# Layer 1's feed-forward: rows sent to one of two experts through DRAM, in place of both experts on all rows

## Chip, core and metric

The kernel runs on one core of one Trainium2 chip. The metric is the device time of one execution in microseconds. A core has five engines with a queue each, all executing in order: PE (TensorE, matrix products), ACT (ScalarE), DVE (VectorE), POOL (GpSimd) and SP (SyncE, which here only issues DMAs). They meet through semaphores.

## The reference

A four-layer decoder on `x` of 128 sequences x 64 rows x 128 features, that is 8192 rows, in float32. Each layer adds a cross-attention over `ctx_1024` and a feed-forward part to `x`, both on the normalised rows. The part that the change touches is layer 1's feed-forward:

```python
gate_scores = xf @ gate_w.T                       # two scores a row
top1 = jnp.argmax(softmax(gate_scores), axis=-1)
one_hot = jax.nn.one_hot(top1, 2)
masked = xf[None, :, :] * one_hot.T[:, :, None]   # a row's copy is zero for the expert it isn't sent to
h = relu(einsum('end,edh->enh', masked, w1) + b1[:, None, :])     # 128 -> 512
expert_out = einsum('enh,ehd->end', h, w2) + b2[:, None, :]       # 512 -> 128
routing_output = expert_out.sum(axis=0)
shared = relu(xf @ sw1 + sb1) @ sw2 + sb2
return routing_output + shared
```

The expert that a row isn't sent to still adds a constant row, `relu(b1) @ w2 + b2`. The other layers: layer 0 mixes eight one-matrix experts densely, layer 2 sends each row to one of seven gated experts beside a shared one, layer 3 has a mixed-projection attention.

## The kernel before

The 8192 rows are 16 groups (`NG`) of 512 rows, each held in SBUF as `xg[g]`, four tiles of 128 rows by 128 features. For each group the program records the operations of six stages: layer 0 attention (`x0`), layer 0 feed-forward (`l0f`), layer 1 attention (`x1`), layer 1 feed-forward (`l1f`), layer 2 attention (`x2`) and layer 2's routing (`route`). Then follow, for two halves of the groups (12 and 4), layer 2's expert blocks (`table`, `block`, `shared`, `gather`) and layer 3 (`l3x`, `mix`, `l3f`).

Nothing runs in recorded order. Each `op(engine, duration, function, reads, writes, priority, ...)` goes into a planner (`Plan`, L162 on), which places all operations of all groups on the five engines by estimated durations, dependencies, buffer slots and priority, and then emits each engine's instructions in that order. The order of every queue is fixed when the program is built. A group's base priority is `10 * g`, plus `SKEW` (15) a stage, plus an offset by stage, operation and engine from the table `PRI`. An operation with `alt` may go to a second engine: normalisation (`ln_xn`, L555), evacuations (`copy_out`, L588) and the rectification in `l1f` go to ACT or DVE, bias rows (`add_row`, L607) to POOL or DVE. So the 16 groups' stages overlap: one group's attention fills the engines while another's feed-forward waits.

Buffers are in pools (`spec`): `c` holds a group's transposed context, `k`, `q` and `o` attention operands, `fx` and `fm` transposed rows, `p` transposed probabilities, `mx` row maxima. `b` is four PSUM banks. `h` is a view of 14 tiles of `hbig`; layer 2's block weights (`wt`) and the hidden tiles `h2` are views of the same storage, and `fw` (3072 columns) holds all of layer 1's weights and, later, layer 2's shared weights. The list `mark["l1f"]` holds the last operations of layer 1's feed-forward; layer 2's weight loads wait for all of them.

`l1f(g)` normalises the rows (`xn`), transposes them (`xnT`), and adds the sum of both experts' and the shared output bias (`add_row`). `logits` gives two scores a row, `choose` (L1095) the 0/1 choice. POOL multiplies `xn` by the choice (L1105), PE transposes the product (`m1T`), and POOL subtracts it from `xnT` (`m0T`, L1115). Then 12 up-projections of 128 hidden features each follow (L1125), over all 512 rows: four of the shared expert on `xnT`, four of expert 1 on `m1T`, four of expert 0 on `m0T`. Each is rectified with its bias (L1134 on ACT, L1136 on DVE) into an `h` tile. For each of the four row tiles, 12 down-projections add up in PSUM (L1144); DVE adds the result to `xg[g]` (L1151).

In attention, the score product reads a key operand (`kbd`) that SP's four DMAs fill from `k` (`fill_kbd`, L652), POOL subtracts the row maximum (`shift`, L794), ACT takes the exponential (L785), PE transposes the probabilities (L809).

Layer 2 already sends rows through DRAM: `route` writes rows with indirect DMAs from POOL into `xs_d` (L1249), `block` loads weights and rows at addresses that SP reads from a table in SBUF (L1410, L1414), and `gather` fetches results with indirect DMAs (L1454).

Of the kernel before, what the change touches and what calls it, by code (L numbers as in the profile page):

```python
# [11 lines left out]
F32 = mybir.dt.float32  # L12
# [31 lines left out]
FW = 3072  # L44
# [15 lines left out]
S_LEN = S_E + E2  # L60
# [5 lines left out]
SKEW, SKEW3, ALT, WINDOW = 15.0, 12.0, 1.160527449, 0.268996472  # L66
# [5 lines left out]
    "block0 block <lambda> 4": -4, "block0 block tr 0": 37, "block0 dma fn 4": 30.5,  # L72
    "block0 swiglu <lambda> 0": 3.5, "block0 swiglu <lambda> 1": 35.5, "block0 swiglu <lambda> 2": -1,
    "block0 swiglu down 0": 20, "block1 block <lambda> 1": 13.5, "block1 block <lambda> 4": -12.5,
    "block1 block tr 0": -22.5, "block1 dma fn 4": 71, "block1 swiglu <lambda> 0": 4,
    "block1 swiglu <lambda> 1": 41, "block1 swiglu <lambda> 2": -32, "block1 swiglu down 0": 1,
    "gather0 gather <lambda> 3": 3.5, "gather0 gather fn 2": 6.5, "gather0 stats fn 2": -0.5,
    "gather1 gather <lambda> 3": 78, "gather1 gather fn 2": 29.5, "gather1 stats fn 2": -3.5,
    "l0f copy_out fn 1": 3, "l0f l0f <lambda> 0": 9, "l0f l0f <lambda> 1": 9.5, "l0f l0f <lambda> 2": -145,
    "l0f l0f acc 2": -123.5, "l0f l0f eb 0": 46.5, "l0f l0f g1 2": 43.5, "l0f l0f g2 2": 41.5,  # L80
    "l0f ln_xn fn 1": 17.5, "l0f logits fn 0": 18.5, "l0f pow_rs fn 3": -4, "l0f stats fn 2": -39,
    "l0f transpose4 fn 0": 59.5, "l1f add_row <lambda> 3": 12.5, "l1f copy_out fn 1": -43.5,
    "l1f l1f <lambda> 0": 196, "l1f l1f <lambda> 2": 55.5, "l1f l1f <lambda> 3": 48, "l1f l1f choose 2": 11.5,
    "l1f l1f down 0": 360, "l1f l1f relu 1": 32, "l1f ln_xn fn 1": -12, "l1f logits fn 0": 5, "l1f pow_rs fn 3": 7,
    "l1f stats fn 2": 0.5, "l1f transpose4 fn 0": 45.5, "l3f0 attend av 0": 41.5, "l3f0 attend tr 0": -4.5,
    "l3f0 copy_out fn 1": -52, "l3f0 dma fn 4": -9.5, "l3f0 exp_ <lambda> 1": 25, "l3f0 fill_kbd fn 4": 56,
    "l3f0 l3f <lambda> 1": 2, "l3f0 l3f <lambda> 2": 17, "l3f0 l3f <lambda> 3": 106, "l3f0 l3f b_v 3": 51.5,
    "l3f0 l3f evac 1": -131, "l3f0 l3f load 4": -2, "l3f0 l3f project 0": -36.5, "l3f0 l3f put 2": -15,
    "l3f0 maximum fn 2": 40, "l3f0 normalise fn 2": 4, "l3f0 out_proj <lambda> 2": 36, "l3f0 out_proj fn 0": 11,
    "l3f0 scores fn 0": -58, "l3f0 shift fn 3": -1, "l3f1 attend av 0": 1, "l3f1 attend tr 0": -22,  # L90
    "l3f1 copy_out fn 1": 8.5, "l3f1 dma fn 4": -3, "l3f1 exp_ <lambda> 1": 14, "l3f1 fill_kbd fn 4": -18,
    "l3f1 l3f <lambda> 1": -2, "l3f1 l3f <lambda> 2": -13.5, "l3f1 l3f <lambda> 3": 4, "l3f1 l3f b_v 3": 9.5,
    "l3f1 l3f evac 1": 12.5, "l3f1 l3f load 4": -13.5, "l3f1 l3f project 0": -58, "l3f1 l3f put 2": -8,
    "l3f1 maximum fn 2": 4, "l3f1 normalise fn 2": -2, "l3f1 out_proj <lambda> 2": 4, "l3f1 out_proj fn 0": -4.5,
    "l3f1 scores fn 0": -26, "l3f1 shift fn 3": -6.5, "l3x0 add_row <lambda> 3": 8, "l3x0 copy_out fn 1": -36,
    "l3x0 dma fn 4": 61.5, "l3x0 l3x <lambda> 1": 166, "l3x0 l3x <lambda> 2": -5.5, "l3x0 l3x <lambda> 3": -10.5,
    "l3x0 l3x av 0": 28.5, "l3x0 l3x norm 2": -21.5, "l3x0 l3x sc 0": 7, "l3x0 l3x sums 2": 33,
    "l3x0 l3x tr 0": -17.5, "l3x0 ln_xn fn 1": 14, "l3x0 pow_rs fn 3": 12, "l3x0 stats fn 2": 9,
    "l3x0 transpose4 fn 0": 15, "l3x1 add_row <lambda> 3": 3.5, "l3x1 copy_out fn 1": -38, "l3x1 dma fn 4": 97,
    "l3x1 l3x <lambda> 1": 36.5, "l3x1 l3x <lambda> 2": 8, "l3x1 l3x <lambda> 3": -2, "l3x1 l3x av 0": 13.5,  # L100
    "l3x1 l3x sc 0": 26, "l3x1 l3x sums 2": -28.5, "l3x1 l3x tr 0": 7.5, "l3x1 ln_xn fn 1": -1,
    "l3x1 pow_rs fn 3": -3, "l3x1 stats fn 2": -1, "l3x1 transpose4 fn 0": -1, "mix0 add_row <lambda> 3": 26.5,
    "mix0 copy_out fn 1": -64, "mix0 ln_xn fn 1": -3.5, "mix0 mix <lambda> 0": 54.5, "mix0 mix <lambda> 1": 18.5,
    "mix0 mix <lambda> 2": -29.5, "mix0 mix b3mm 0": 37.5, "mix0 mix choose 2": 81, "mix0 mix put 2": 27.5,
    "mix0 mix spread_ 0": 101, "mix0 mix weigh 2": -76, "mix0 pow_rs fn 3": -17.5, "mix0 transpose4 fn 0": 38,
    "mix1 add_row <lambda> 3": 42, "mix1 copy_out fn 1": -14.5, "mix1 ln_xn fn 1": 3.5, "mix1 mix <lambda> 0": 16,
    "mix1 mix <lambda> 1": 10.5, "mix1 mix <lambda> 2": -26.5, "mix1 mix b3mm 0": 1.5, "mix1 mix choose 2": 5.5,
    "mix1 mix put 2": 28, "mix1 mix spread_ 0": 15.5, "mix1 mix weigh 2": -25.5, "mix1 pow_rs fn 3": 2.5,
    "mix1 transpose4 fn 0": -0.5, "route copy_out fn 1": -98.5, "route dma fn 4": 0.5, "route ln_xn fn 1": 51.5,
    "route pow_rs fn 3": 13, "route route <lambda> 1": 2, "route route <lambda> 2": -25,  # L110
    "route route <lambda> 3": 48.5, "route route count 0": -3, "route route r2 2": -22, "route route r3 2": 8,
    "route route r4 2": 11.5, "route route r5 2": -1.5, "route route take 2": -4.5, "route stats fn 2": -19.5,
    "route transpose4 fn 0": 7, "shared0 copy_out fn 1": 10.5, "shared0 ln_xn fn 1": 10.5,
    "shared0 shared fn 2": 11.5, "shared0 swiglu <lambda> 0": 11, "shared0 swiglu <lambda> 1": 8.5,
    "shared0 swiglu <lambda> 2": 7, "shared0 swiglu down 0": 20.5, "shared0 transpose4 fn 0": 3.5,
    "shared1 copy_out fn 1": -16, "shared1 ln_xn fn 1": 24, "shared1 shared fn 2": -7,
    "shared1 swiglu <lambda> 0": 11, "shared1 swiglu <lambda> 1": -2.5, "shared1 swiglu <lambda> 2": 1,
    "shared1 swiglu down 0": 6.5, "shared1 transpose4 fn 0": 21.5, "table0 table <lambda> 0": 26,
    "table0 table b1 2": -3.5, "table0 table b2 2": 28, "table1 table <lambda> 0": 16, "table1 table b1 2": 2,
    "table1 table b2 2": 9.5, "x0 add_row <lambda> 3": 27, "x0 attend av 0": -6, "x0 attend tr 0": 9.5,  # L120
    "x0 attention <lambda> 2": -1.5, "x0 attention <lambda> 3": 26, "x0 copy_out fn 1": -102, "x0 dma fn 4": 504.5,
    "x0 exp_ <lambda> 1": -9, "x0 fill_kbd fn 4": -5, "x0 ln_xn fn 1": 19.5, "x0 maximum fn 2": 70,
    "x0 normalise fn 2": -88.5, "x0 out_proj <lambda> 2": -40.5, "x0 out_proj fn 0": -25.5, "x0 pow_rs fn 3": 4,
    "x0 proj <lambda> 0": 32.5, "x0 proj fn 1": -32, "x0 scores fn 0": 12, "x0 shift fn 3": -2,
    "x0 stats fn 2": -30, "x0 transpose4 fn 0": 10, "x0 vproj evac 1": -2, "x0 vproj fn 0": 73,
    "x1 attend av 0": 33, "x1 attend tr 0": 6.5, "x1 attention <lambda> 2": -35, "x1 attention <lambda> 3": 11,
    "x1 copy_out fn 1": -28.5, "x1 dma fn 4": 501.5, "x1 exp_ <lambda> 1": 10, "x1 fill_kbd fn 4": 5,
    "x1 ln_xn fn 1": 95.5, "x1 maximum fn 2": 10.5, "x1 normalise fn 2": -46.5, "x1 out_proj <lambda> 2": -103,
    "x1 out_proj fn 0": -1, "x1 pow_rs fn 3": 2, "x1 proj <lambda> 0": 24, "x1 proj fn 1": -1,
    "x1 scores fn 0": 83.5, "x1 shift fn 3": -14, "x1 stats fn 2": -15.5, "x1 transpose4 fn 0": 8,  # L130
    "x1 vproj evac 1": -1, "x1 vproj fn 0": 9.5, "x2 add_row <lambda> 3": 0.5, "x2 attention <lambda> 2": -46,
    "x2 attention <lambda> 3": 90.5, "x2 copy_out fn 1": -11.5, "x2 dma fn 4": 506, "x2 fill_kbd fn 4": 3.5,
    "x2 ln_xn fn 1": -3, "x2 out_proj <lambda> 2": -34, "x2 out_proj fn 0": -0.5, "x2 pow_rs fn 3": 8,
    "x2 product fn 0": -45, "x2 proj <lambda> 0": -13, "x2 proj fn 1": -9.5, "x2 scores fn 0": -13,
    "x2 stats fn 2": -15.5, "x2 transpose4 fn 0": 29, "x2 vproj_by_batch evac 2": -93.5,
    "x2 vproj_by_batch fn 0": -44, " b2_row b2_row 2": 2.5, " dma fn 4": 497, " lambda <lambda> 0": 32.5,
    " lambda <lambda> 2": -29.5, " lambda <lambda> 3": 14.5, " rel_mm rel_mm 0": -11.5,
# [162 lines left out]
def kernel(ctx: ExitStack, tc: tile.TileContext, a: dict, out: bass.AP):  # L300
# [90 lines left out]
    def tl(r):  # L391
        return kinds[r.tag][r.slot]
# [1563 lines left out]
```

## Time and profile before

| | us |
|---|---|
| median of 21 runs | 1990.86 |
| lowest and highest of them | 1983.95, 1999.85 |
| the profiled execution | 1993.57 |
| span of its instructions | 1991.8 |
| POOL's indirect scatter (L1249), mean of 64 | 0.989 |
| POOL's indirect gather (L1454), mean of 64 | 1.004 |
| rectification of 128x512 on ACT (L1134), mean of 164 | 0.685 |
| the same on DVE (L1136), mean of 28 | 0.741 |

Engine times in the text are of this one execution. A "group" of the profile is all instructions with the same line, engine and tiles; its row gives their busy time and the mean of one. In rows with a bar the first number after it is busy time, the second the mean in ns, the last part the idle time of the engine just before them and what ended it.

### The profile page before, as it was taken

Reading aid. Unit: us, or ns where it says so; the run is one execution under the profiler, and the core shown is the slowest. Engines: PE = TensorE matmul, PEld = TensorE weight load, DVE = VectorE, ACT = ScalarE, POOL = GpSimd, SP = SyncE. Lnnn points to the kernel's source line nnn. Section 1 sums busy time; section 2 is a strip of 40 time slices with the busy share of each in tenths; the row PEclk is TensorE's granted clock in tenths of the full one; section 3 lists DMA queues with packets and bytes.
Section 4 is the critical chain, followed back from the end, with each engine's and each line's share of the span. In section 5 each row is a group of like instructions: output and inputs, shape, how many; then the busy total and the mean of one; then the engine's idle time right before and its main releaser. Section 6 shows DMA issues by size and latency. Waiting matters only on the chain.

```text
span 1991.8 us, 66420 instructions
## 1 busy us (share of the span) xinstructions
PE 1807.9 (91%) x27506; PEld 1305.3 (66%) x27506; DVE 1547.7 (78%) x4023; ACT 1083.0 (54%) x2032; POOL 1021.0 (51%) x1331
## 2 busy tenths in 40 slices
PE   7778999999998999999999999999998987888885
PEld 5544756765765666765666667778756776676664
DVE  5989897878798987798987864445577878988666
ACT  2545755555555565556564553343445666666554
POOL 5635745464555654557644471020388768855231
PEclk8989999999999999999999999999999999989898
DMA  6200001011001010001001012444424576545461
GB/s 186 80 13 26 27 26 30 13 30 40 24 29 46 28 32 29 27 27 50 29 24 33 23 42 79 133 128 121 121 75 127 155 245 188 172 151 178 158 190 54
DMA packets 139229, 158.73 MB, mean 80 GB/s; under 512 B 40836, under 2 KB 98096, under 8 KB 138928
## 3 DMA queue, kind: packets, MB, share of 16 engines
q1 hardware_dynamic: 134832, 146.09, 24.1%
q0 software_dynamic: 4096, 8.40, 1.5%
q8 instruction: 216, 3.54, 0.7%
q14 instruction: 85, 0.70, 0.1%
HBM read 121.66 MB, written 15.99 MB: 69 GB/s over the span
## 4 chain that ended last, share of the span: by engine, by line
PE 48%; DVE 26%; POOL 8%; issue 8%; ACT 4%; DMA 3%; SPq 3%; POOLq 0%; DVEq 0%; ACTq 0%
PE b L1353 8%; PE b L1144 5%; PE b L809 4%; POOL s L794 4%; DVE x L1078 4%; PE b L1125 4%; PE b L1382 4%; DVE mx L779 4%; PE S L755 4%; PE b L1068 3%; PE b L638 3%; PE b L821 2%; PE b L1734 2%; PE b L864 2%; PE b L583 2%
## 5 line engine op out<-in xcount | busy, mean ns | idle before, releaser
L794 POOL TENSOR_TENSOR s<-s,mx 128x512 f32<-128x512 f32 x320 | 323.7, 1044 | 224.9 <-DVE mx L779 187.7
L593 ACT COPY p<-b 128x512 f32<-128x512 f32 x370 | 199.0, 591 | 144.4 <-PE b L809 127.6
L809 PE MATMUL b<-ident,s 128*128 128x128 f32 x1536 | 216.5, 291 | 48.7 <-ACT s L785 35.0
L785 ACT ACTIVATE s<-s 128x2048 f32<-128x2048 f32 x96 | 183.8, 1914 | 111.2 <-POOL s L794 82.3
L809 PEld LDWEIGHTS b<-ident,s 128*128 128x128 f32 x1536 | 180.2, 149 | 93.1 <-ACT s L785 54.0
L563 ACT ACTIVATE xn<-x,nmr,rstd 128x128 f32<-128x128 f32 x472 | 194.4, 488 | 26.2 <-POOL nmr L548 24.9
L1078 DVE SCALAR_TENSOR_TENSOR x<-b,gt,x 128x128 f32<-128x128 f32 x512 | 177.9, 347 | 30.2 <-PE b L1068 13.9
L544 POOL TENSOR_SCALAR ve<-mv 128x4 f32<-128x4 f32 x144 | 34.8, 242 | 320.0 <-DVE mv L538 305.0
L755 PE MATMUL S<-kbd,q 32*64 32x256 f32 x4096 | 151.7, 401 | 46.4 <-DMA kbd<-k 22.5
L1144 PEld LDWEIGHTS b<-fw,hbig 128*128 128x128 f32 x1536 | 178.0, 192 | 10.4 <-issue 9.4
L779 DVE TENSOR_REDUCE mx<-s 128x32 f32<-128x2048 f32 x80 | 181.8, 2274 | 3.5 <-ACT s L1786 2.9
L1144 PE MATMUL b<-fw,hbig 128*128 128x128 f32 x1536 | 183.9, 277 | 0.0
L1370 DVE TENSOR_TENSOR hbig<-fm,b 128x256 f32<-128x256 f32 (+2 forms) x180 | 85.3, 486 | 101.2 <-ACT fm L1365 74.5
L1134 ACT ACTIVATE hbig<-b,cols 128x512 f32<-128x512 f32 x164 | 111.3, 685 | 84.2 <-PE b L1125 83.4
L1068 PE MATMUL b<-mats,fx 128*128 128x512 f32 x256 | 140.0, 629 | 1.8 <-DVE x L1078 1.5
L545 POOL TENSOR_TENSOR rstd<-ve,mhalf 128x4 f32<-128x4 f32 x128 | 133.6, 1044 | 10.7
L755 PEld LDWEIGHTS S<-kbd,q 32*64 32x64 f32 x4096 | 82.2, 136 | 86.8 <-DMA kbd<-k 21.9
L1353 PE MATMUL b<-fx,hbig 128*128 128x256 f32 (+1 forms) x528 | 128.9, 393 | 4.2 <-ACT fx L1441 1.0
L1365 ACT ACTIVATE fm<-b 128x256 f32<-128x256 f32 (+2 forms) x180 | 76.5, 438 | 100.8 <-PE b L1353 92.0
L821 PEld LDWEIGHTS b<-p,vaug 128*32 128x32 f32 x6144 | 97.9, 112 | 50.0 <-issue 24.3
L821 PE MATMUL b<-p,vaug 128*32 128x64 f32 x6144 | 124.1, 226 | 6.3 <-issue 4.1
L1125 PE MATMUL b<-fm,fw 128*128 128x512 f32 x256 | 125.1, 606 | 0.6 <-DVE x L1078 0.3
(292 smaller groups left out, 3870.6 us busy)
## 6 DMA issues: line engine op xcount, KB each, us to landing
fw<-in_l_w SPq DMA_DIRECT2D x64, 384.0 KB
vaug<-in_l_w SPq DMA_DIRECT2D x64, 384.0 KB
hbig<-in_l_w SPq DMA_DIRECT2D x44, 544.0 KB
c<-in_ctxT SPq DMA_DIRECT2D x64, 256.0 KB
kbd<-k SPq DMA_DIRECT2D x256, 64.0 KB
q<-xs_d SPq DMA_DIRECT2D x44, 128.0 KB
ys_d<-o SPq DMA_DIRECT2D x44, 128.0 KB
x<-in_x SPq DMA_DIRECT2D x32, 128.0 KB
```

What stands on the lines that cost most here:

```text
L563: A.activation(y[:, t, :], xg[g][:, t, :], AF.Identity, bias=nmr[:, g, n], scale=rstd[:, g, n])
L593: A.copy(tl(dst), tl(b))
L755: T.matmul(ps[64 * i : 64 * i + 64, r, u * 256 : u * 256 + 256], lhsT=qT[row, 64 * b : 64 * b + 64], rhs=kbd[row, :, 64 * b : 64 * b + 64] ...
L779: V.tensor_reduce(tl(mxr), heads(y), AX.X, ALU.max)
L794: G.tensor_tensor(y, y, bc(tl(mxr)[:, h], 2, [P, n, S]), ALU.subtract)
L809: T.transpose(tl(b)[:, r * P : (r + 1) * P], tl(s)[:, c : c + P], ident)
L821: T.matmul(tl(po)[32 * r : 32 * r + 32, c : c + 64], lhsT=vaugs[kv.slot][:, w0 : w0 + 32], rhs=tl(ps[p])[:, r * P + 64 * i : r * P + 64 * ...
L1068: lambda t=t, u=u, pe=pe: T.matmul(tl(pe), lhsT=tl(xnT)[:, t * P : (t + 1) * P], rhs=mats[:, M_E0 + 4 * u : M_E0 + 4 * u + 4, :], start=Tr ...
L1078: V.scalar_tensor_tensor(xg[g][:, t, :], tl(pe)[:, e * D : (e + 1) * D], w[:, t, 4 * u + e : 4 * u + e + 1], xg[g][:, t, :], ALU.mult, ALU ...
L1125: lambda n=n, src=src, ph=ph: T.matmul(tl(ph), lhsT=fw[:, n * P : (n + 1) * P], rhs=tl(src), start=True, stop=True),
L1144: T.matmul(tl(py)[:, t * P : (t + 1) * P], lhsT=tl(hs[n])[:, t * P : (t + 1) * P], rhs=w2f[:, n, :], start=(n == 0), stop=(n == 11),)
L1353: T.matmul(tl(ps)[0:n, at : at + m], lhsT=w()[:, off + c * P : off + c * P + n], rhs=tl(xT)[:, 0:m], start=True, stop=True,)
```

## The change

Layer 1's feed-forward is cut in three. Groups are taken in pairs (1024 rows).

- `l1f(g)` normalises and transposes as before. `choose` now also finds each row's place: rows for expert 0 count from the start of a 1024-row DRAM tile (`x1_d`), rows for expert 1 from its end. A count matmul ranks rows across partitions, `place` writes the addresses, and four indirect DMAs on POOL scatter the normalised rows. On the odd group of a pair, `table1` works out which of the first four blocks of 256 rows is whose. `unsent` adds the constant difference row `cd`, made once in `zeros`, to the rows whose unsent expert is expert 0. The shared expert (4 up, 16 down) runs on `xnT` at once (`up_down`).
- `l1b(n)` runs five blocks of 256 rows for pair `n`. SP reads the block's expert from the table, loads that expert's weights (128 x 1028) and the rows; two transposes, four ups, four rectifications, eight downs; ACT copies the result and SP stores it to `y1_d`. Four blocks cover the tile in order, and the fifth is the block in which the two experts meet, computed a second time with expert 1.
- `l1c(g)` fetches the results with four indirect DMAs and adds them to `xg[g]` on POOL or DVE.

Stages `x2` and `route` of both groups of a pair are recorded after the pair's `l1c`. The table `PRI` (shortened away below), `ALT` and `WINDOW` hold other numbers, some of the planner's durations differ, the loads of `tri` and `srt` have priority 16 in place of 40, and several pools are of other sizes.

```diff
-FW = 3072
+FW = 3080
+HID1, B1 = 512, 256
+N1 = 2 * GT
+NB1 = N1 // B1 + 1
+W1 = HID1 + 4 * D + 4
...
-SKEW, SKEW3, ALT, WINDOW = 15.0, 12.0, 1.160527449, 0.268996472
+SKEW, SKEW3, ALT, WINDOW = 15.0, 12.0, 1.493905422, 0.159761594
...
-        "c": (2, [P, GT]), "q": (2, [P, GT]), "k": (3, [P, GT]), "o": (3, [P, GT]),
-        "xnT": (1, [P, GT]), "xn": (2, [P, GT]), "fx": (2, [P, GT]), "fm": (4, [P, GT]), "p": (5, [P, GT]),
-        "s": (2, [P, 2048]), "m": (2, [P, 256]), "mb": (3, [P, 256]), "mx": (12, [P, 32]), "tn": (1, [P, 288]),
-        "st": (4, [P, TP * 6]), "gt": (2, [P, 264]),
-        "rt": (1, [P, 400]),
+        "c": (1, [P, GT]), "q": (2, [P, GT]), "k": (2, [P, GT]), "o": (3, [P, GT]),
+        "xnT": (1, [P, GT]), "xn": (2, [P, GT]), "fx": (4, [P, GT]), "fm": (3, [P, GT]), "p": (4, [P, GT]),
+        "s": (2, [P, 2048]), "m": (2, [P, 256]), "mb": (2, [P, 256]), "mx": (6, [P, 32]), "tn": (1, [P, 288]),
+        "st": (7, [P, TP * 6]), "gt": (3, [P, 264]),
+        "rt": (2, [P, 400]),
...
+    kinds["w1"] = [fw[:, HID1 + 4 * D + i * W1 : HID1 + 4 * D + (i + 1) * W1] for i in range(2)]
...
     def l1f(g, pri):
         xn, xnT = layer_norm(g, pri, "fx")
         add_row(g, R_B20, pri)
...
+            V.tensor_copy(pos.unsqueeze(2), gs[:, :, 0:1])
+            V.tensor_tensor(sel.unsqueeze(2), gs[:, :, 1:2], pos.unsqueeze(2), ALU.is_gt)
+            V.tensor_copy(on, sel)
+            V.tensor_tensor(
+                y, srt[:, S_TRI : S_TRI + 20].rearrange("p (i t) -> p i t", t=TP), bc(on, 1, [P, 5, TP]), ALU.mult
+            )
+            V.tensor_reduce(pre, y, AX.X, ALU.add)
...
+        def count():
+            T.matmul(tl(rank)[:, 0:1], lhsT=tri, rhs=pre[:, 4:5], start=True, stop=not k)
...
+        def place():
+            V.tensor_tensor(pos, pos, tl(rank)[:, 0:1].to_broadcast([P, TP]), ALU.subtract)
+            V.tensor_copy(ip.bitcast(I32), pos)
...
+        def scatter(t):
+            w = G.indirect_dma_start(
+                out=x1_d[n], out_offset=bass.IndirectOffsetOnAxis(ap=ip[:, t : t + 1].bitcast(I32), axis=0),
+                in_=g4(tl(xn))[:, t, :], in_offset=None,
+            )
...
+            G.memset(scrap, 0.0)
...
+        def unsent():
+            for t in range(TP):
+                V.scalar_tensor_tensor(xg[g][:, t, :], cd, sel[:, t : t + 1], xg[g][:, t, :], ALU.mult, ALU.add)
...
+    def l1b(n, pri):
...
+        for j in range(NB1):
+            wt, xb, xbT = Res("w1"), Res("q"), Res("fx")
+            last = j == NB1 - 1
+
+            def weights(j=j, wt=wt, last=last):
+                at = P if last else register(tab1[0:1, n, j : j + 1], P)
+                SY.dma_start(out=tl(wt), in_=a["l1_we"][bass.ds(at, P), :])
+
+            def rows_in(j=j, xb=xb, last=last):
+                at = register(tab1[0:1, n, 4:5], N1 - B1) if last else j * B1
+                SY.dma_start(
+                    out=view(tl(xb)[:, 0:B1]), in_=x1_d[n][bass.ds(at, B1), :].rearrange("(t p) d -> p t d", p=P)
+                )
...
+    def l1c(g, pri):
+        yg = Res("k")
+        for t in range(TP):
+            op(
+                POOL, 1.0,
+                lambda t=t: G.indirect_dma_start(
+                    out=g4(tl(yg))[:, t, :], out_offset=None, in_=y1_d[g // 2],
+                    in_offset=bass.IndirectOffsetOnAxis(ap=l1cell(g, L_YP + t, 1).bitcast(I32), axis=0),
+                ),
...
+    for g in range(NG):
+        stats(g, 10.0 * g - 0.5)
+        stages(g, enumerate((0, l0f, 1, l1f)))
+        if g % 2:
+            plan.stage = "l1b"
+            l1b(g // 2, 10.0 * g + SKEW * 3 + 3)
+            for i in (g - 1, g):
+                plan.stage = "l1c"
+                l1c(i, 10.0 * g + SKEW * 3 + 6)
+                stages(i, ((4, 2), (5, route)))
```

The up- and down-projections, for the shared expert (`m` = 512) and for a block (`m` = 256):

```python
    def up_down(xT, m, w1, w2, b1, wr, take, pri):
        hs = []
        for c in range(4):
            ...
                lambda c=c, ph=ph: T.matmul(tl(ph)[:, 0:m], lhsT=w1(c), rhs=tl(xT)[:, 0:m], start=True, stop=True),
            ...
            def relu(e, c=c, h=h, ph=ph):
                if e == ACT:
                    A.activation(tl(h)[:, 0:m], tl(ph)[:, 0:m], AF.Relu, bias=b1(c))
                else:
                    V.tensor_scalar(tl(h)[:, 0:m], tl(ph)[:, 0:m], b1(c), 0.0, ALU.add, ALU.max)
            ...
        def down():
            for t in range(m // P):
                for c in range(4):
                    T.matmul(
                        tl(py)[:, t * P : (t + 1) * P], lhsT=tl(hs[c])[:, t * P : (t + 1) * P], rhs=w2(c),
                        start=(c == 0), stop=(c == 3),
                    )
        op(PE, 0.92 * m / P, down, r=[*hs, wr], w=[py], pri=pri, mode="f")
        mark.setdefault("l1f", []).append(plan.ops[-1])
        take(py)
```

## The prediction

> **What bounds the kernel now.** I read the page's busy shares and slices first, then the busy times by stage, then the groups of layer 1's feed-forward, then the chain of waits.
>
> ```profile
> span 1991.8 us, 66420 instructions
> PE 1807.9 (91%) x27506; PEld 1305.3 (66%) x27506; DVE 1547.7 (78%) x4023; ACT 1083.0 (54%) x2032; POOL 1021.0 (51%) x1331
> PE   7778999999998999999999999999998987888885
> DVE  5989897878798987798987864445577878988666
> ```
>
> TensorE (PE) leads in most slices, but the vector engine (DVE) is close behind it in the first 23. A share of the whole span says little, so the next view cuts it where the work changes: the last down-projection of layer 1 is issued at 1217 us, and the blocks of layer 2 start there.
>
> ```profile
> 50.00:200.00 150.00, 121.70 (x1650) 73.02 (x1640) 139.16 (x370) 75.77 (x126) 78.84 (x111) 0.92 0.13 39
> 200.00:1000.00 800.00, 765.11 (x12203) 520.67 (x12202) 684.76 (x1645) 456.34 (x803) 452.00 (x577) 1.00 0.10 31
> 1000.00:1217.00 217.00, 209.16 (x3211) 149.30 (x3210) 156.92 (x384) 108.37 (x189) 103.54 (x136) 0.99 0.09 28
> 1217.00:1450.00 233.00, 231.48 (x1887) 179.91 (x1886) 115.83 (x360) 104.63 (x247) 42.09 (x65) 1.00 0.42 123
> ```
>
> Columns: window, length, busy time of PE, weight load, DVE, ACT, POOL, then clock, DMA share, GB/s. From 200 to 1217 us PE is busy 974.3 of 1017 us (96%) and DVE 841.7 (83%). From 50 to 200 us it is the other way round: DVE is busy 92.8%, PE 81%. That stretch shows how full DVE gets when it is the one that is short. Call 0 to 1217 us stage A: PE 1131.2, DVE 1008.0, ACT 655.2, POOL 659.9. All of layer 1's feed-forward lies in A.
>
> ```profile
> L1144 PE MATMUL b<-fw,hbig 128*128 128x128 f32 x1536 | 183.9, 277 | 0.0
> L1125 PE MATMUL b<-fm,fw 128*128 128x512 f32 x256 | 125.1, 606 | 0.6 <-DVE x L1078 0.3
> L1125 PE MATMUL b<-fx,fw 128*128 128x512 f32 x128 | 64.1, 606 | 0.0
> L1078 DVE SCALAR_TENSOR_TENSOR x<-b,gt,x 128x128 f32<-128x128 f32 x512 | 177.9, 347 | 30.2 <-PE b L1068 13.9 <-ACT q L646 1.5
> L1249 POOL DMA_INDIRECT xs_d<-p,rt x64 | 63.3, 989 | 120.7 <-ACT p L563 109.4 <-issue 10.1 <-ACT fm L1365 0.4
> ```
>
> ```profile
> 1072.17 5.36 PE b L1125 x12
> 1205.33 5.36 PE b L1144 x48
> 1244.22 2.59 PE b L1353 x12
> ```
>
> The means of the groups overlap their neighbours, so PE's price is taken from back-to-back runs in the chain. Each matmul leaves two records: six of 512 columns took 5.36 us (0.893 each), 24 of 128 columns 5.36 (0.223), six of 256 columns 2.59 (0.432).
>
> **PE, part by part.** Counts are the instructions in each kernel's own order. Gone: 192 up-projections of 512 columns (171.5 us), 768 down-projections (171.3), 64 transposes of the masked rows (103.0 us over 640 in the transposes' group, 0.161 each: 10.3). Together 353.1. Added: 64 up-projections for the shared expert (57.2), 160 of 256 columns (69.1), 256 + 320 down-projections (128.4), 80 transposes of loaded blocks (17.4 us over 88 in layer 2's blocks, 0.198 each: 15.8), 40 one-column counting matmuls and 8 for the zero rows. No row has one column; between nothing and the 226 ns of a 64-column one (L821) lie 0 to 11 us; I take 5. Sum 276. PE loses 77 us and A needs 1054.
>
> **DVE.** Gone: the three short operations of the choice (0.32 for the transpose, two at 0.19, as the 128x4 to 128x32 rows have: 11.2 us for 16 groups) and 28 rectifications (0.741 each, 20.7). Added: the choice now has nine (29.4), the place two (6.1), the table of each pair 13 (8 x 13 x 0.19 = 19.8), the correction of unsent rows 64 at 0.347 to 0.414 (L1078, L1464; I take 0.36: 23.0), rectifications 9 x 0.741 and 40 x 0.416 (23.3), two of the final additions (1.5). The planner moves work off DVE: 20 normalisations fewer (0.376), 5 evacuations (0.685), 6 projections (0.75), four bias rows and four copies more: -11. Sum +60, so A needs 1068.
>
> So DVE takes PE's place as the fuller engine of A. That is the core of the forecast: the saving is not PE's 77 us.
>
> **ACT and POOL.** ACT: 192 rectifications and 15 evacuations become 175 shorter rectifications and 80 block copies; 112.3 + 8.8 go, 37.7 + 45.7 + 29.7 and 20 normalisations (9.8) come: about +2 on 655, hidden. POOL: the mask multiply and the subtraction go (16.6 + 20.4). 64 scatters with their guard memset (0.989 + 0.117: 70.8), 64 gathers (1.004 each: 64.3) and 14 additions (1.27: 17.8) come, four bias rows go. Net +111, A needs 771, some 65% of it: hidden as a sum. What queues behind a waiting scatter or gather on POOL is the softmax subtraction (L794), for which ACT's exponential and then PE wait; that is a rival below.
>
> ```profile
> L1249 POOL DMA_INDIRECT xs_d<-p,rt x64: 954/958/1424, 608.8 to 1426.5; - x64
> DMA to landing us min/median/max: 2.2/2.7/5.1
> ```
>
> The indirect transfers keep a narrow price while DVE is busy: minimum, median and maximum are 954, 958 and 1424 ns. If all 128 cost the maximum, POOL would have 60 us more, 831 in all, still covered.
>
> Here a rule speaks against the change. The Trainium skill's page "SBUF — State Buffer" (section "SBUF: two separate sides") says that descriptors of a DMA issued from POOL cannot be written while DVE holds the shared port pair in a two-port operation; its next section gives 620 ns alone against 3100 ns overlapped. By that, as an estimate from the page, 128 transfers could cost 317 us more on POOL and make POOL the bound. The row above shows no case near 3100 ns.
>
> **SP and the DMAs.** 40 weight loads (128x1028 words, 526 KB), 40 row loads and 40 stores join SP's queue with 40 register loads. At 0.35 to 0.46 us an issue (L1414, L413 rows) and 0.27 a register load that is some 60 us of issue, among key fills that PE needs (L656). The bytes, some 39 MB in A, meet a DMA share of 0.10 to 0.13. I cost both at nothing while the planned order covers latency. Between a pair's count and its first block's transposes the changed order has 20, 38, 18, 21, 20, 25, 15 and 11 us of other PE work (priced from the rows of before). The chain needs two short DVE operations (0.4), four scatters (5.0 with issue), landing (2.7) and a row load, nearest row the same 2.7: 11 us. Seven pairs are covered, the last just.
>
> **Two losses.** The last pair's five blocks must end before any layer-2 block may load its weights (both use the same storage, and the `l1f` mark holds them). They are 5 x (2 transposes, 4 up, 8 down) = 5 x 3.9 = 20 us of PE work with an evacuation between the steps. Bounds: 0 if the other groups' layer-2 attention fills the gaps, 20 if nothing does; it fills half of that stretch in the order, and I take 5. Smaller pools (one context buffer for two, two `k` for three, four `p` for five) can delay key fills: PE waited 22.5 us on these in the whole span, so 0 to 22; I take 5. A retuned priority table also moves work both ways; a gain is not excluded, and the same 22 us bounds it below nothing.
>
> **Sum.** If DVE keeps A as full as it kept 50 to 200 us, A ends at 50 + (1068 - 27.2)/0.928 = 1172 instead of 1217: -45. With the two losses -35. After A the counts of DVE and PE hardly change and PE is 99% busy in the next window in both, so the shift carries through. The profiled execution took 1993.57 (1991.8 of it the span): 1958. It lies 2.7 above the median of 1990.86, so the forecast is 1955.
>
> **Rivals.** (1) PE stays the only bound and DVE follows: A shrinks by its whole 77 us, and the time is 1990.9 - 77 = 1914. For it: from 550 to 600 us both engines are above 91% at once. Against: DVE would need 1041/1090 = 95% for the whole stage.
>
> (2) DVE fills A only to 0.89: A ends at 1219, 2 us later than before, and with no loss added the time is 1993. For it: with PE the bound it is at 0.856 from 200 to 1000 us. Against: it was never the short engine there.
>
> (3) Slower: the hand-over of each pair stalls the in-order queues. The mechanism is the wait of SP's row load, or POOL's gather, for transfers through DRAM, with key fills and the softmax subtraction behind it. The trace has it once:
>
> ```profile
> SPq L1414 <- DMA xs_d<-p,rt: 14.1, 1, 14.1
> ```
>
> Once per pair that is 113 us; if half reaches PE, 56 - 35 = +21: 2012. It decides from 35/8 = 4.4 us per pair. Against: the cover counted above, and waits for block loads in layer 2 that hide behind PE work.
>
> That five blocks run always, whatever the split, is already in the counts (10240 expert rows for 16384); no skipping is assumed.
>
> **Chances.** Forecast 0.50, rival one 0.20, two 0.12, three 0.18. Within 0.2% is about what a measurement here can't tell from no change (4 us); rival two gives 0.05 faster, 0.04 same, 0.03 slower. Faster 0.75, same 0.04, slower 0.21. The forecast's own range is 1920 to 1985: 1920 with A filled to 0.95 (it ends at 1146) and no loss, 1985 with 0.91 (1194) and losses of 17. To leave out no more than 2 in 10 it reaches down to the first rival, 1910, and up to the third, 2010.
>
> **What would show it.** Layer 1's up and down matmuls near 255 us of PE instead of 343; the last of them issued near 1180 us; DVE above 90% busy from 200 us to there, PE below it or equal; POOL near 65%; indirect transfers near 0.96 us; weights' and rows' loads without PE waits. Wrong if DVE stays below 87% there while PE waits on DMA or POOL (rival three), or if the tail after A grows.

## The result and the profile after

| | before | after |
|---|---|---|
| median | 1991.57 us (56 runs, 1983.95 to 1999.85) | 2054.34 us (8 runs, 2044.49 to 2058.21) |
| profiled execution, span, mean granted clock | 1993.57, 1991.8, 0.971 | 2042.02, 2040.3, 0.953 |
| last down-projection of layer 1 (end of stage A) | 1217 us | 1233 us |

The changed kernel is slower: after/before is 1.0312 [1.0296, 1.0328], some 62 us. The forecast was 1955 and its range ended at 2010. The page of the profile after, its busy times and three rows of its 40 slices:

```profile
span 2040.3 us, 67280 instructions
PE 1780.0 (87%) x27298; PEld 1301.1 (64%) x27298; DVE 1622.0 (79%) x4320; ACT 1100.8 (54%) x2170; POOL 1127.4 (55%) x1496
...
PE   6878799999899988988898998999998878888886
...
DVE  5999999889789888889886784554557889989865
...
PEclk7899999999999999999999999999999988989898
```

DVE has 74 us more, POOL 106 more, PE only 28 less. The busy times by stage of the same kernel (window, length, PE, weight load, DVE, ACT, POOL, clock, DMA share, GB/s):

```profile
50.00:200.00 150.00, 122.36 (x1719) 77.82 (x1718) 140.62 (x394) 75.60 (x123) 90.72 (x134) 0.91 0.13 38
200.00:1000.00 800.00, 722.00 (x11455) 497.84 (x11453) 702.27 (x1788) 443.00 (x820) 490.96 (x633) 0.97 0.22 64
1000.00:1233.00 233.00, 209.49 (x3319) 149.49 (x3319) 185.66 (x503) 121.72 (x245) 147.69 (x201) 0.98 0.25 73
1233.00:1490.00 257.00, 248.39 (x2254) 189.53 (x2253) 129.03 (x388) 120.47 (x281) 52.07 (x80) 0.99 0.37 111
```

From 200 to 1000 us PE now is busy 90% (before 96%) at a clock of 0.97 (before 1.00), and DVE 88% (before 86%). Neither engine is full, and the stage is longer all the same: 16 us at its end, and 32 us more behind it. Before, PE's largest sum of waits from 200 to 1217 us was this one (what waited, for what: us in total, times, longest):

```profile
PE b L809 <- ACT s L785: 8.6, 15, 1.3
```

After, from 200 to 1233 us, several waits for DVE stand near the top:

```profile
PE b L881 <- issue: 10.7, 7, 2.7
PE b L826 <- ACT s L802: 10.2, 8, 3.5
PE b L655 <- DVE x L1209: 5.8, 2, 5.3
PE b L826 <- DVE x L1095: 5.2, 2, 4.3
PE b L1220 <- DVE hbig L1228: 4.9, 6, 1.5
PE S L772 <- DMA kbd<-k: 4.5, 6, 1.3
...
PE b L1166 <- DVE l1s L1160: 3.3, 4, 1.7
```

All rows of the two views together: 40 us of waits before, 18 of them for DVE, and 97 us after, 53 of them for DVE. L1209 adds the shared expert's result to the rows, behind the correction of the unsent rows; L1160 ends the choice, L1166 is the counting matmul. How one such wait comes about, on the timeline of the kernel after (start, us, engine, line, operation, and in brackets the idle time before it and its releaser):

```profile
229.84 4.04 POOL L811 TENSOR_TENSOR s<-s,mx 128x512 f32<-128x512 f32 x4 [7.64 <-DVE l1s L1179]
...
231.95 0.96 DVE L1262 SCALAR_TENSOR_TENSOR l1t<-l1t,l1s 128x8 f32<-128x8 f32 x1
...
232.95 0.97 DVE L1263 TENSOR_TENSOR l1t<-l1t,l1s 128x8 f32<-128x8 f32 x1
...
242.51 3.52 DVE L1203 SCALAR_TENSOR_TENSOR x<-cd,l1s,x 128x128 f32<-128x128 f32 x4
242.74 4.19 POOL L811 TENSOR_TENSOR s<-s,mx 128x512 f32<-128x512 f32 x4 [1.14 <-DVE mx L796]
...
246.16 0.69 DVE L1209 TENSOR_TENSOR x<-x,b 128x512 f32<-128x512 f32 x1
...
246.91 2.07 PE L655 MATMUL b<-xnT,mats 128*128 128x512 f32 x2 [5.29 <-DVE x L1209]
```

The four corrections take 3.52 us beside POOL's subtraction, L1209 follows, and PE's next projection (L655), of an attention, stands 5.29 us until it is done. No normalisation or transpose lies between the two; L1209 reads a PSUM bank (`b`) and L655 writes one, so the wait fits one for a free bank.

### The profile page after: what moved, and what is told of

Read it like the earlier page. It is cut to its first block, busy times and chain, and to the rows that moved or that the text cites. A ratio compares the mean times of both kernels' runs of the same rounds, so it can differ in the third digit from the quotient of the medians.

```text
span 2040.3 us, 67280 instructions
## 1 busy us (share of the span) xinstructions
PE 1780.0 (87%) x27298; PEld 1301.1 (64%) x27298; DVE 1622.0 (79%) x4320; ACT 1100.8 (54%) x2170; POOL 1127.4 (55%) x1496
## 3 DMA queue, kind: packets, MB, share of 16 engines
q8 instruction: 215, 3.52, 0.7%
## 5 line engine op out<-in xcount | busy, mean ns | idle before, releaser
L811 POOL TENSOR_TENSOR s<-s,mx 128x512 f32<-128x512 f32 x320 | 324.0, 1045 | 255.2 <-DVE mx L796 183.3
L826 PE MATMUL b<-ident,s 128*128 128x128 f32 x1536 | 228.3, 299 | 64.4 <-ACT s L802 38.4
L826 PEld LDWEIGHTS b<-ident,s 128*128 128x128 f32 x1536 | 186.8, 153 | 116.3 <-ACT s L802 56.1
L580 ACT ACTIVATE xn<-x,nmr,rstd 128x128 f32<-128x128 f32 x492 | 202.2, 489 | 48.2 <-POOL nmr L565 45.6
L1220 PE MATMUL b<-fx,fw 128*128 128x256 f32 (+1 forms) x448 | 159.4, 469 | 12.6 <-DVE hbig L1228 4.9
L1238 PE MATMUL b<-fw,hbig 128*128 128x128 f32 x1152 | 141.8, 278 | 3.5 <-DVE hbig L1228 1.7
L1238 PEld LDWEIGHTS b<-fw,hbig 128*128 128x128 f32 x1152 | 134.2, 192 | 15.9 <-issue 7.7
L1554 ACT ACTIVATE fm<-b 128x256 f32<-128x256 f32 (+2 forms) x180 | 76.7, 438 | 108.1 <-PE b L1542 89.4
L553 DVE BATCH_NORM_STATS2 st<-x 128x6 f32<-128x128 f32 x512 | 110.4, 278 | 15.9 <-DMA x<-in_x 8.6
```

What stands on the lines that cost most here:

```text
L580: A.activation(y[:, t, :], xg[g][:, t, :], AF.Identity, bias=nmr[:, g, n], scale=rstd[:, g, n])
L811: G.tensor_tensor(y, y, bc(tl(mxr)[:, h], 2, [P, n, S]), ALU.subtract)
L826: T.transpose(tl(b)[:, r * P : (r + 1) * P], tl(s)[:, c : c + P], ident)
L1220: lambda c=c, ph=ph: T.matmul(tl(ph)[:, 0:m], lhsT=w1(c), rhs=tl(xT)[:, 0:m], start=True, stop=True),
L1238: T.matmul(tl(py)[:, t * P : (t + 1) * P], lhsT=tl(hs[c])[:, t * P : (t + 1) * P], rhs=w2(c), start=(c == 0), stop=(c == 3),)
```

## The experiments

A ratio is to the kernel before, run in the same set. In two sets the kernel before itself took 2037 us, so there only the ratio counts, and differences of such a set are taken inside it. Differences in us are between medians where nothing else is said. Three sorts: plans exchanged, work taken out or added with the order of the instructions kept, and one try at a better kernel.

### Other plans: pools and tables of priorities

Before with after's storage pools:

```diff
-        "c": (2, [P, GT]), "q": (2, [P, GT]), "k": (3, [P, GT]), "o": (3, [P, GT]),
-        "xnT": (1, [P, GT]), "xn": (2, [P, GT]), "fx": (2, [P, GT]), "fm": (4, [P, GT]), "p": (5, [P, GT]),
+        "c": (1, [P, GT]), "q": (2, [P, GT]), "k": (2, [P, GT]), "o": (3, [P, GT]),
+        "xnT": (1, [P, GT]), "xn": (2, [P, GT]), "fx": (4, [P, GT]), "fm": (3, [P, GT]), "p": (4, [P, GT]),
...
```

> The kernel before with the changed kernel's pool sizes and nothing else (one context buffer, two k, four p, six mx, and so on). Theory pools (the smaller pools delay loads and key fills): most of the 62 us, 2020 or more. Theory route (the routed feed-forward itself costs the time) and theory order (the other priority table costs it): within 12 us of 1991.

Measured 1.0573 [1.0535, 1.0611], 114 us of 2037.07: more than the whole loss that it was to explain.

Before with after's priorities for every stage but layer 1's feed-forward (`b_prio`), after with before's priorities there (`a_prio`), both with the other kernel's `ALT` and `WINDOW` too, and after with before's priorities for layer 2's blocks and what follows alone (`a_late`):

```diff
-PRI = {...}
+PRI = {**own entries for l1f, l1b, l1c, zeros, **the other kernel's for the rest}
```

> The kernel before with the changed kernel's priorities for every stage but the feed-forward of layer 1, and its ALT and WINDOW. Theory order: 2030 or more. Theory route: a table fitted to other work does some harm, but under 20 us: 1991 to 2010. Theory pools: as route.

Measured 1.0579 [1.0546, 1.0611].

> The changed kernel with the priorities, ALT and WINDOW of before for every stage but the feed-forward of layer 1. Theory order: the loss goes with the table, 2010 or less. Theory route: 2045 or more, since the waits of the routed rows stay. Theory pools: 2045 or more.

Measured 1.1528 [1.1491, 1.1564].

> The changed kernel with the priorities of before for the blocks, table, shared expert and gather of layer 2 and for layer 3 only. The span from 1233 us on was 32 us longer than before's from 1217 us on. Theory order: this part shrinks by 20 to 30 us, 2025 to 2035. Theory route or pools: 2045 or more, since the later stages are long because work was left over from the first.

Measured 1.1039 [1.0984, 1.1093].

Both kernels with no priorities at all, `a_flat` with before's `ALT` and `WINDOW` too:

```diff
-PRI = {...}
+PRI = {}
```

> The kernel before with an empty priority table (every offset 0). b_prio and a_prio showed that a table fitted to other work costs 6 to 15%. Theory order: both kernels owe much to their tables; this one loses 6 to 12%.

Measured 1.0807 [1.077, 1.0844], 2148.28 us.

> The changed kernel with an empty priority table and the ALT and WINDOW of before, so that neither kernel's order is fitted. Theory order (the routed feed-forward is the better algorithm, and its fitted order is worse than before's): faster than b_flat by 2 to 4%. Theory route: slower than b_flat by 3% or more.

Measured 1.1497 [1.1465, 1.1529], 2283.75 us.

All these ratios are to before, so those of `a_prio`, `a_late` and `a_flat` contain after's own 1.0312. Against the kernel that it was made from, every one of these plans costs some 6 to 12%, more than the whole effect, so exchanging plans can't single out a cause. One thing remains of it: without priorities the routed kernel, with its own pools, is 6.3% slower than the dense one (2283.75/2148.28), so its loss is not that of an unlucky table. What single parts cost has to be asked of a kernel whose order stays as it is.

### PE's work alone, order kept

`b_cut` is before without one of the three groups of four chunks of the up- and down-projections (chunks 0 to 3 are left out):

```diff
-                lambda n=n, src=src, ph=ph: T.matmul(
+                lambda n=n, src=src, ph=ph: n < 4 or T.matmul(
...
+                if n < 4:
+                    return
...
-                for n in range(12):
+                for n in range(4, 12):
```

> The kernel before with every instruction in its place, but expert 0's up-projections, rectifications and down-projections not issued: 114 us of PE work (64 x 0.893 + 256 x 0.223) leaves the first stage, and the output lacks that expert. The forecast's model (PE bounds the stage, then DVE at 0.928): 95 to 114 us less. Theory chain (the waits between engines set the stage and this PE work fills gaps): 20 to 60 less.

A third of 343 us of matmuls is gone, 114 us. Measured 0.9984 [0.9967, 1.0001], 5 us of 1987.44, less than either theory had. By stage, in the columns of before:

```profile
200.00:1000.00 800.00, 711.05 (x11754) 479.32 (x11742) 674.99 (x1633) 431.32 (x761) 449.37 (x574) 0.97 0.10 30
1000.00:1210.00 210.00, 183.45 (x3012) 128.06 (x3012) 156.99 (x384) 98.03 (x174) 104.86 (x138) 0.96 0.10 30
```

PE is busy 89% where it was 96%, DVE as much as before, and DVE's own schedule stayed where it was. Two of its lines (count: minimum, median and maximum ns, first and last start): the mixing of layer 0's experts and layer 1's additions to the scores, first in before, then in `b_cut`:

```profile
L1078 DVE SCALAR_TENSOR_TENSOR x<-b,gt,x x512: 306/351/370, 81.8 to 1067.1; 128x128 f32<-128x128 f32 x171
L978 DVE TENSOR_TENSOR s<-S,bias x32: 2250/2281/2293, 134.8 to 1118.6; 128x2048 f32<-128x2048 f32 x32
```

```profile
L1078 DVE SCALAR_TENSOR_TENSOR x<-b,gt,x x512: 306/351/360, 82.3 to 1068.2; 128x128 f32<-128x128 f32 x171
L978 DVE TENSOR_TENSOR s<-S,bias x32: 2252/2280/2292, 134.4 to 1117.5; 128x2048 f32<-128x2048 f32 x32
```

The last of them starts 1 us later and 1 us earlier. So PE's 96% was no limit in this order: layer 1's projections filled time in which PE would otherwise have stood. Two things stay open. The granted clock fell with the work, from 1.00 to 0.97; PE still stood idle 11% of the stretch, but what the same cut is worth at an unchanged clock no run shows. And with the order kept no other work can move into the time that is freed; what a plan made for less PE work would gain was not tried.

### DVE's work alone, order kept

`b_dve` is before with ten more operations of 128x128 behind each group's addition of layer 1's result, which leave the rows as they are:

```diff
-        op(DVE, 0.69, lambda: V.tensor_tensor(xg[g], xg[g], g4(tl(py)), ALU.add), r=[py], w=[X[g]], pri=pri)
+        def add_(py=py):
+            V.tensor_tensor(xg[g], xg[g], g4(tl(py)), ALU.add)
+            for i in range(10):
+                V.scalar_tensor_tensor(xg[g][:, i % 4, :], g4(tl(py))[:, i % 4, :], 0.0, xg[g][:, i % 4, :], ALU.mult, ALU.add)
```

> The kernel before with ten more DVE operations a group after layer 1's feed-forward (each adds zero times the PSUM result to a tile of x: 160 x 0.347 = 55 us of DVE in the first stage), every other instruction in its place. The forecast's model: DVE would need 1063 us, at 0.928 up to 1166, below 1217, so 0 to 15 us more. Theory chain: DVE's time is passed on, 30 to 55 more.

Measured 1.0116 [1.009, 1.0141], +23 us by the ratio (24.8 by medians). What was added is smaller than 160 times the 0.347 us of L1078. The added operations in `b_dve` (busy us in all, mean ns of one, idle before):

```profile
L1155 DVE SCALAR_TENSOR_TENSOR x<-b,x 128x128 f32<-128x128 f32 x160 | 33.1, 280 | 0.6
```

33 us added to an engine that is busy 83% in this stage came out as 23 us, 70% (the 42% of a later expectation are 23 of the 55 us that were expected). The last addition to layer 1's scores starts at 1144.3 us in its trace instead of 1118.6. DVE's idle time did not take it up. That this is time in which a layer's chain of operations is on another engine fits, but is argued. The run prices DVE's time at one place only: the ten operations stand between a group's result and its next normalisation, and they read the result's PSUM bank and so keep it longer. Which of the two passes the time on was not separated.

### What the routed part costs, order kept

`a_again` is the changed kernel once more. `b_noexp` is before without both routed experts (no choice, mask, masked transposes; chunks 8 to 11, the shared expert's, stay). `a_noroute` is after without all that is routed; only the shared expert stays. From it the parts are put back one after the other: in `a_book` the choice, count, place, table and correction; in `a_noblock` also the scatters; in `a_nogather` also the blocks; gathers and last additions make it `a_again`. `a_nounsent` is after without the correction alone. `a_choose` has of the routed part the choice alone, `a_place` the choice, count and place. Each skips operations when the planned order is written out, by name:

```diff
-            o.emit()
+            if not o.name.startswith(skip):
+                o.emit()
+# a_noroute: l1b, scatter, l1c, count, place, table1, unsent, choose
+# a_book: l1b, scatter, l1c      a_noblock: l1b, l1c
+# a_nogather: l1c                a_nounsent: unsent
+# a_choose: l1b, scatter, l1c, unsent, table1, count, place
+# a_place: l1b, scatter, l1c, unsent, table1
```

> The changed kernel once more, on the chip of the next three, so that they can be set beside it: 3.0 to 3.3% above before.

> The kernel before with every other instruction in its place, but neither expert issued (no choice, mask multiply, second transposes, subtraction, expert projections or rectifications; the output lacks both). b_cut took 114 us of PE work away for 5 us. Theory chain: 10 to 30 us less than before, 1960 to 1980. If PE bounded the stage it would be 200 less.

> The changed kernel with every other instruction in its place, but nothing of the experts issued (no choice, count, place, table, scatters, correction of unsent rows, blocks, gathers, additions; the output lacks both). It computes what b_noexp does, so the two differ by order and pools alone. Theory route (the routed part itself costs the time): within 15 us of b_noexp, 60 to 80 us below a_again. Theory order (the other table and pools): 35 us or more above b_noexp, at most 40 below a_again.

> The changed kernel with every other instruction in its place, but the correction of unsent rows (64 DVE operations, 25.4 us) not issued; rows of expert 1 get another constant row. b_dve passed on 42% of added DVE time: 8 to 14 us less than a_again. Theory order: the same, since it says nothing of DVE.

> First step of a ladder from a_noroute (1976.8) to the changed kernel (2053.8), every other instruction in its place. Issued: choice, count, place, table and the correction of unsent rows; left out: scatters, blocks, gathers and final additions (the output lacks the experts). Theory DVE: the short DVE operations and the correction bring 25 to 40 us. Theory queues (POOL's indirect transfers and the waits on DRAM are the cost): under 20.

> Second step: a_book with the 64 scatters on POOL issued; blocks, gathers and final additions left out. Theory queues: the scatters, 71 us of POOL before the softmax subtractions, bring 15 to 30 us. Theory DVE: under 10.

> Third step: a_noblock with the 40 blocks issued; only gathers and final additions are left out. Block work on PE fills gaps, as the dense experts' did: 5 to 15 us by both theories, of which DVE's 40 rectifications (18 us) give some 8. What is then left to 2053.8 is the gathers': theory queues 20 or more, theory DVE 10 or less.

> Between a_noroute (0.9932 of before) and a_book (1.0175): of the bookkeeping only the choice is issued, nine short DVE operations a group (some 27 us of DVE in all); no count, place, table or correction (the output lacks the experts). Theory DVE time: 42 to 60% of it, 11 to 16 us above a_noroute. Theory hop (the way DVE, PE, DVE of count and place is the cost): the same 11 to 16, and the rest in the next run.

> a_choose with count and place as well (two more short DVE operations a group, 7 us, behind one-column matmuls on PE). Theory DVE time: 3 to 5 us above a_choose. Theory hop: 12 us or more above it, since DVE stands before place until PE has counted. What is left to a_book is the table (25 us of DVE) and the correction (25 us, 12.5 in a_nounsent).

Measured; PE, DVE and POOL are busy us of the profiled execution, and the last column is the start of the last addition to layer 1's scores on DVE (L978, L995 or the line that it has become):

| | ratio | median (before) | PE | DVE | POOL | last score add |
|---|---|---|---|---|---|---|
| before | 1 | | 1807.9 | 1547.7 | 1021.0 | 1118.6 |
| `b_noexp` | 0.9885 [0.9845, 0.9924] | 1969.88 (1990.64) | 1646.0 | 1524.2 | 983.5 | 1109.2 |
| `a_noroute` | 0.9932 [0.9912, 0.9952] | 1976.79 (1990.64) | 1652.3 | 1527.7 | 972.8 | 1090.3 |
| `a_choose` | 0.9888 [0.9863, 0.9914] | 2010.74 (2036.24) | 1656.7 | 1548.3 | 972.5 | 1096.1 |
| `a_place` | 0.9904 [0.9878, 0.9929] | 2014.83 (2036.24) | 1671.2 | 1554.5 | 972.5 | 1100.3 |
| `a_book` | 1.0175 [1.0142, 1.0208] | 2022.70 (1991.61) | 1664.2 | 1603.2 | 974.1 | 1121.2 |
| `a_noblock` | 1.0174 [1.0141, 1.0208] | 2023.44 (1991.61) | 1668.7 | 1600.5 | 1043.6 | 1124.5 |
| `a_nogather` | 1.0269 [1.0237, 1.03] | 2041.90 (1991.61) | 1782.4 | 1619.6 | 1043.8 | 1144.3 |
| `a_nounsent` | 1.0266 [1.023, 1.0301] | 2041.28 (1990.64) | 1784.4 | 1603.2 | 1125.2 | 1144.7 |
| `a_again` | 1.0334 [1.0299, 1.0369] | 2053.79 (1990.64) | 1780.9 | 1627.4 | 1126.8 | 1149.2 |

The dense experts cost before 21 us (1990.64 - 1969.88), though they are some 229 us of matmuls; of DVE they have 24 us (1547.7 - 1524.2). The routed ones cost after 77 us (2053.79 - 1976.79), with 100 us of DVE. With neither, the two orders differ by 7 us, and their intervals overlap. So 77 - 21 + 7 = 63, the whole loss (the sum holds by construction; what it tells is the size of its parts).

Of the 77, by medians: choice to correction 46 (the two kernels are of different sets, both with before near 1991), scatters 0.7, blocks 18.5, gathers and additions 12 (again two sets). The step of 46 has 75.5 us more on DVE, 12 on PE and 1 on POOL, so 61% of DVE's time came through, near `b_dve`'s 70%; in us it is above the 25 to 40 that were expected. The correction alone is 12.5 us for 24 us of DVE. The blocks bring 114 us of PE, 76 of ACT and 19 of DVE, and cost 18.5, more than the 5 to 15 expected: at 52 to 70% their DVE time would be 10 to 13 of it. The gathers with their additions cost 12, between what the two theories had, with 8 us of DVE and 83 of POOL. What the rest of these two steps waits for was not separated. The scatters bring 70 us of POOL and nothing measurable.

Count and place, with their way from DVE to PE and back, cost 4.1 us (`a_place` against `a_choose`, one set, intervals overlap) for 6 us of DVE: the 12 or more that the theory of the hop had did not come. But `a_choose` can't be set beside `a_noroute`: its ratio is lower (0.9888 against 0.9932) though it does more, against both theories, so a ratio from the set with before at 2036 us does not seem to carry over to one with 1991. The last column can be read across sets with some care, since each is one execution (after twice: 1147.4 and 1149.2). It puts choice at 6, count and place at 4, table and correction at 21, scatters 3, blocks 20, gathers 5: 59 of the 77 us are there by the end of layer 1's attention. How the 46 us split between choice, table and correction is not settled by medians.

What became of PE's freed time, in the windows of `a_noroute`:

```profile
200.00:1000.00 800.00, 675.74 (x11219) 438.16 (x11217) 673.67 (x1606) 415.78 (x727) 420.98 (x543) 0.93 0.10 31
```

and of `a_book`:

```profile
200.00:1000.00 800.00, 656.41 (x11015) 429.28 (x11014) 704.23 (x1800) 403.52 (x703) 410.13 (x524) 0.94 0.10 29
```

PE is at 82 to 84% in both, with hardly any PE work between them (40 matmuls of one column, 80 records); `a_book` has 31 us more on DVE in the same 800 us and has got less far (11015 matmul records against 11219).

### A try at a faster kernel

If DVE is the chain, work moved from it to ACT, which is busy 54%, should help. `b_act` is before with all operations of layers 0 and 1 and of layer 2's first part that may run on either engine put on ACT:

```diff
+        early = ("x0", "x1", "x2", "l0f", "l1f", "route")
         for o in plan.order():
+            if o.eng == DVE and ACT in o.durs and o.name.startswith(early):
+                o.eng = ACT
             o.emit()
```

> The kernel before with every instruction in its place, but the normalisations, evacuations and rectifications that the planner gave to DVE in layers 0 to 2 (some 80 us there) issued on ACT. Theory chain with DVE at its centre: 42% of the time taken off DVE is gained, less what ACT, 54% busy, hands on: 10 to 35 us faster than before. Rival: the planner gave them to DVE where ACT was late, so ACT's lateness replaces DVE's: no gain or slower.

Measured 1.0068 [1.0045, 1.0092], 12 us slower. The page of `b_act`:

```profile
PE 1809.4 (90%) x27506; PEld 1302.8 (65%) x27506; DVE 1477.1 (74%) x3870; ACT 1145.0 (57%) x2185; POOL 1020.3 (51%) x1331
```

DVE lost 71 us and the time rose; the last addition to the scores starts at 1126.2 us, 8 later. So DVE is no plain bound either. From 200 to 1217 us PE's waits for DVE fell from 18.1 to 11.2 us against before, and those for ACT rose from 9.7 to 20.8: the lateness went over to ACT with the work, as the rival had it. None of the kernels that were run beats before with the work complete.

## Why the prediction was wrong

**The step that failed** is "So DVE takes PE's place as the fuller engine of A", with its sum "A ends at 50 + (1068 - 27.2)/0.928 = 1172 instead of 1217". It treats stage A as a tank that its fullest engine empties, so that PE's 77 us are free to gain until DVE is full. The runs show a chain in its place: 114 us less on PE gave 5 us, 33 us more on DVE gave 23 lost, at 83% busy. A busy share of 96% says that PE was given work to fill its waits, not that something waits for PE. DVE stayed near the fill it had (from 200 to 1000 us 86% before, 88% after, forecast 0.928), and the stage became longer instead. In this order PE's saving was worth almost nothing, and DVE's increase, which the sum counted only where DVE would become the bound, was most of the price: at the 61% of the bookkeeping, the routed part's 100 us of DVE would be 61 of its 77 us. The other 16, in the blocks and gathers, have no shown cause.

**PE, -77.** PE's work went down, but its busy time in all fell by only 28 us (1807.9 to 1780.0), while the granted clock fell from 0.971 to 0.953. The groups of layer 1 in the profile after (busy us, mean ns, idle before):

```profile
L1238 PE MATMUL b<-fw,hbig 128*128 128x128 f32 x1152 | 141.8, 278 | 3.5 <-DVE hbig L1228 1.7 <-ACT hbig L1226 1.5
...
L1220 PE MATMUL b<-fx,fw 128*128 128x256 f32 x320 | 92.7, 405 | 8.5 <-DVE hbig L1228 4.5 <-DVE rt L1372 1.1 <-ACT hbig L1226 0.5
L1220 PE MATMUL b<-fx,fw 128*128 128x512 f32 x128 | 67.0, 630 | 4.1 <-ACT hbig L1226 3.1 <-DVE hbig L1228 0.4 <-DVE x L1095 0.3
```

The prediction named some 255 us for these; the groups, which overlap their neighbours, add to 301, where before had 373 by the same view: 72 us less, not the 88 of the forecast.

**DVE, +60.** Right in kind, and near in size: up to the end of A 1008.0 became 1056.1, over the whole span +74. The correction was the best hit in work, 23.0 forecast and 25.4 measured, though not as foreseen (see the last section).

**ACT +2, POOL 771.** ACT 655.2 became 651.9 and POOL 659.9 became 751.9, both hidden, as `a_noblock` shows for the scatters. The gathers with their additions are not free: 12 us.

**Indirect transfers at 0.96 us.** Right. The two lines after, minimum, median and maximum ns:

```profile
L1185 POOL DMA_INDIRECT x_d<-xn,l1s x64: 955/965/1320, 179.9 to 1192.3; - x64
L1330 POOL DMA_INDIRECT k<-y_d,l1s x64: 941/948/1115, 345.9 to 1261.2; - x64
```

The Trainium skill's page "SBUF — State Buffer" (section "SBUF: two separate sides") has the descriptors of such a transfer wait while DVE runs a two-port operation, and the prediction put 3100 ns on one that waits. None of the 128 is above 1320 ns, with DVE 88% busy, so no run here shows a wait of that size.

**SP and the covers.** Held for the time: key fills are 4.5 us of PE's waits in A. SP's queue stood 51.1 us in seven waits for the table (L1275 behind DVE's L1268), 16.8 us in four for the scattered rows, and 108.1 us in 23 for the down-projections (L1238) that free a weight buffer for the next load (L1290). All of PE's waits for DMAs from 200 to 1233 us are 5.2 us. **Smaller pools** can't be told apart: before with after's pools lost 5.7%, but with an order made for other ones.

**Two losses, 5 + 5.** Not seen as such; 32 of the 48 us in the profiled executions arise behind stage A, and the prediction had named a growing tail as a sign of being wrong. "After A the counts of DVE and PE hardly change" was right for the counts (DVE 1532 and 1544 operations), but their busy time grew, PE's from 676.7 to 694.0 us and DVE's from 539.7 to 565.9, and PE, forecast at 99%, was busy 97% in the window behind A. Layer 2's first gather starts at 1502.9 us instead of 1431.7, 71 later where A's end is 16 later. The profiled executions without experts tell what of this is the order's. At the last addition to layer 1's scores after's order is 19 us ahead of before's (`a_noroute` 1090.3, `b_noexp` 1109.2), and at the end 7 us behind it (spans 1980.4 and 1973.1): it loses 26 us between the two. The routed experts add 59 us by that addition and 12 more behind it, the dense ones of before 9 and 9. So `a_again` loses 29 us against before behind that point: 26 of the order and 12 of the routing, less the dense experts' 9. The order had gained 19 ahead of it. Each of these is one execution.

**The rivals.** One (1914) took PE for the only bound, and `b_cut` contradicts it directly. Two (1993) had the right direction, a DVE less full, but kept the same picture. Three (2012) had the right sign by a wrong place: the scatters cost 0.7 us, and PE hardly waits for DMAs; a share of the hand-over in the 12 us of the gathers is not excluded. Most of the loss was in the forecast's own row of DVE.

## What to carry to other kernels

Before a saving on the busiest engine is counted, leave that work out with the order kept and see whether the other engines' last instructions move: an engine at 96% that nothing waits for is filling gaps. Here work added to the engine through which each layer's results pass came through at 52 to 70% of its time, though that engine is idle a sixth of the time; many small bookkeeping operations are dear there and large matmuls in the gaps are cheap. A plan that was fitted to one kernel is worth 6 to 12% in it, so compare parts with the order held, and keep in mind that a held order can't use what it saves.

## What the hardware did unexpectedly

**The granted clock fell where PE had less to do.** From 200 to 1000 us it was 1.00 in before, 0.97 in `b_cut` and 0.93 in `a_noroute`, and PE was busy 96, 89 and 84%. In `b_cut` PE's busy time fell by 81 us over the span where 114 us of work were taken out. With poorer plans the same 27506 records take longer: 1881.4 us of PE at a clock of 0.936 in `b_prio`, 1807.9 at 0.971 in before. Busy time multiplied by clock is 1761 and 1755, so the clock would account for that difference.

**Some of DVE's operations took several times their median, and those fall beside POOL's elementwise work.** In the profile after, the correction and an operation of the table, minimum, median and maximum ns:

```profile
L1203 DVE SCALAR_TENSOR_TENSOR x<-cd,l1s,x x64: 309/344/4529, 179.5 to 1198.3; 128x128 f32<-128x128 f32 x64
L1263 DVE TENSOR_TENSOR l1t<-l1t,l1s x8: 166/168/967, 232.9 to 1189.3; 128x8 f32<-128x8 f32 x8
```

On the timeline above, the 0.96, 0.97 and 3.52 us all fall beside POOL's subtraction (L811), whose four pieces take 4.04 and 4.19 us as they do elsewhere (a piece has a mean of 1.045 us). Both engines' operands lie in SBUF there. Over the whole trace, five of the 64 corrections take more than 1 us, and all five overlap an elementwise operation of 128x512 on POOL (four L811, one L1338); of the other 59, at most 409 ns each, two do. Of the eight L1263, two take 967 ns and both overlap L811; the other six overlap none and take at most 235. That POOL's operation is the cause was not tried by itself.
